# First token tile loaded in halves over two DMA queues, mixing factors turned between filler products, decay and bias turned by VectorE

## The chip, the cores and the metric

The kernel runs on one core of a Trainium2 chip. A core has five engines with a queue of instructions each: TensorE (PE in the profile; its weight loads are PEld), VectorE (DVE), ScalarE (ACT), GpSimd (POOL) and SyncE (SP). Engines run side by side and wait for each other by semaphores. TensorE multiplies and writes to PSUM[...]. Data come from HBM by DMA. A DMA is issued by an engine's queue, here that of SyncE or ScalarE, and is carried out by 16 DMA engines that both queues share.

The metric is the device time of one execution in microseconds; lower is better.

## The reference

The input `x` has 4 sequences of 1024 tokens with 512 features, in float32. One layer is computed: a normalization, a recurrent "time mix" part and a feed-forward part, both on the normalized tokens, added to `x`. Cut to what matters:

```python
xn = layernorm(x)

# time mix
xx = concat([xn[:, 1:2], xn[:, :-1]], axis=1) - xn     # token before, minus token
k = (xn + xx * time_mix_k) @ Wk.T                      # 512 -> 704
r = (xn + xx * time_mix_r) @ Wr.T                      # 512 -> 704
w = exp(-exp(time_decay))
state_t = state_{t-1} * w + relu(k_t)                  # along the tokens
a = layernorm((state_t * r_t) @ Wv.T) * ln_gamma + ln_beta

# feed-forward
D = gelu(float16(xn) @ W0.T + bias0).astype(float16)   # 512 -> 2048
E = (D @ W1.T + bias1).astype(float16)                 # 2048 -> 512
out = x + a + E
```

In the kernel `time_mix_k` and `time_mix_r` are the mixing factors, `time_decay` and `bias0` the decay and the bias of the title. Each is a vector along features or hidden units, stored in HBM as a row; the kernel needs it as a column, one value in each partition, so it loads rows and turns them.

## The kernel before

The 4096 tokens are worked on in 8 blocks of 512 tokens. Within a block, features and hidden units lie on the partitions and tokens along the free axis, so a block's normalized tokens must be turned (transposed) first. A block is then the `k` and `r` products (`pk`, `pr`, five chunks of 128 hidden units and a half chunk), the scan over the tokens on VectorE, the product with `Wv` (`po`), and 16 chunks of the feed-forward part (`pd` up, `pe` down). A block's normalization and turning run beside the block before it; TensorE then has products from one block to the next.

The first block has nothing to run beside. `first_inputs` (line 233) does its start by hand: TensorE, VectorE and ScalarE run there in the order in which the lines are written (`tc.manual_schedule`, line 311). The block is cut into four slices `s` of 128 tokens, one for each of the four tiles that `load_x` loads. The steps are:

- **Loads.** `load_x` (line 80) issues on SyncE's queue two tiles of 128 tokens (256 KB each), then four pieces of `wk`, the first three chunks' columns (line 98), then the other two tiles. The rest of `wk` follows (line 128), then `wr` (130), the first pieces of `W0` (150), `Wv`, gamma, beta and `bias1` (180 to 185), and the next block's tiles (87). Each DMA of a queue waits until an earlier one has released its semaphore; there are 8 of these, handed out in turn over both queues. On ScalarE's queue are the mixing factors (123, 124), 4 rows each into `mix_rows`, then the decay (125, 126) and the bias (127), 22 rows in all, into `late_rows`. After these, ScalarE loads the table of the square root (315).
- **Filler.** `busy(n)` (line 249) issues `n` products of zeros into a PSUM tile that nobody reads, `idle`. A float32 product takes two passes on TensorE, so ten of them are 20 matmul records.
- **First slice.** VectorE takes mean and variance of slice 0 (263, 264), ScalarE the root (265). VectorE then does the statistics of slice 1 (266), the reciprocal (267) and the normalization of slice 0 in two pieces, 128 columns and 384 (`normalized`, line 206). Slice 1 gets its statistics in full at line 270 and its root from GpSimd (196, 197).
- **Factors.** TensorE turns `mix_rows` into the PSUM tile `small` after the ten fillers (317). ScalarE copies it to `mix_sb` and makes one minus the factors (319, 320).
- **Turning and mixing.** `turned(s)` (line 276) turns a slice with four transposes into the PSUM tiles `pt`. `mixed` makes the mixed input `xk` of each feature chunk `c`: ScalarE scales (292), VectorE adds the token before (297). `products` (307) then multiplies each chunk with three chunks of `wk`; these go into `pk_0` to `pk_2`.
- **Late rows.** TensorE turns `late_rows` into `small` too, after `turned(0)` (322). ScalarE copies them to `late_sb` after the first slice's mixing (338) and makes `w` from the decay with two exponentials (340, 341), ahead of which it loads another table.

The loop over the slices (327 to 343) puts the turning of slice `s + 1` ahead of the last chunk's products of slice `s`, and the statistics of slice `s + 2` at the end of slice `s`. After it come the `r` inputs of all 512 tokens (345), and from there on a scheduler sets the order, with a few waits that the code adds.

Of the kernel before, what the change touches and what calls it, by code (L numbers as in the profile page):

```python
# [10 lines left out]
F32 = mybir.dt.float32  # L11
# [4 lines left out]
P = 128  # L16
# [4 lines left out]
def time_mix_and_gelu_ffn(  # L21
# [26 lines left out]
    nc = tc.nc  # L48
# [4 lines left out]
    NS = TB // P  # L53
    NC = C // P
    NN = N // P
    Q = 32


    NF = HID // P
    H0 = NF * P  # L60
    HF = P // 2
# [3 lines left out]
    def pool(name, bufs, **kw):  # L65
        return ctx.enter_context(tc.tile_pool(name=name, bufs=bufs, **kw))
# [4 lines left out]
    const = pool("const", 1)  # L71
# [8 lines left out]
    def load_x(i, amid=lambda: None):  # L80

        b, t0 = blocks[i]
        xs = one.tile([P, NS, C], F32, tag="x", name=f"x_{i}")
        for s in range(NS):
            if s == NS // 2:
                amid()
            nc.sync.dma_start(xs[:, s, :], x[b, t0 + s * P : t0 + (s + 1) * P, :])
        return xs


# [5 lines left out]
    def load_wk(cols):  # L96
        for c in range(NC):
            nc.sync.dma_start(wk_sb[c][:, cols], wkT[c * P : (c + 1) * P, cols])

    x_now = load_x(0, lambda: load_wk(slice(0, FIRST * P)))  # L100
    ident = const.tile([P, P], F32, name="ident")
    make_identity(nc, ident)
    nhalf = const.tile([P, NS], F32, name="nhalf")
    nc.vector.memset(nhalf, -0.5)


    eps_sb = const.tile([P, 1], F32, name="eps_sb")
    nc.vector.memset(eps_sb, EPS)

# [2 lines left out]
    rest_sb = const.tile([P, 2 * NC], F32, name="rest_sb")  # L112
    mk_sb, mr_sb = mix_sb[:, :NC], mix_sb[:, NC:]
    ND = NF + 1
    late_rows = const.tile([ND + NN, P], F32, name="late_rows")
    nc.vector.memset(late_rows[:, HF:], 0.0)
    late_sb = const.tile([P, ND + NN], F32, name="late_sb")
    w_sb, b0_sb = late_sb[:, :ND], late_sb[:, ND:]

    def rows(ap):  # L120
        return ap.rearrange("(c p) -> c p", p=P)

    nc.scalar.dma_start(mix_rows[:NC], rows(mix_k))
    nc.scalar.dma_start(mix_rows[NC:], rows(mix_r))
    nc.scalar.dma_start(late_rows[:NF], rows(decay[:H0]))
    nc.scalar.dma_start(late_rows[NF:ND, :HF], decay[H0:].rearrange("(c p) -> c p", p=HF))
    nc.scalar.dma_start(late_rows[ND:], rows(bias0))
    load_wk(slice(FIRST * P, HID))
    for c in range(NC):
        nc.sync.dma_start(wr_sb[c], wrT[c * P : (c + 1) * P, :])  # L130
# [61 lines left out]
    def rstd_of(var, name):  # L192

        n = var.shape[1]
        r = two.tile([P, n], F32, tag=f"rstd{n}", name=name)
        nc.gpsimd.tensor_scalar_add(r, var, EPS)  # L196
        nc.gpsimd.tensor_tensor(r, r, nhalf[:, :n], ALU.pow)
        return r

    def stats_of(mv, s, src, name):  # L200
        st6 = two.tile([P, 6], F32, tag="st6", name=name)
        nc.vector.bn_stats(st6, src)  # L202
        nc.vector.bn_aggr(mv[:, s, :], st6)  # L203

    def normalize(dst, src, mean, rstd):
        nc.vector.tensor_scalar(dst, src, mean, rstd, ALU.subtract, ALU.mult)
# [21 lines left out]
    def product(dst, w, cols, src, c):  # L228
        return nc.tensor.matmul(  # L229
            dst, w[c][:, cols], src, start=(c == 0), stop=(c == NC - 1)  # L230
        )

    def first_inputs(xs, behind):

        pts = [ps_e.tile([P, TB], F32, tag="pe", name=f"pt_0_{c}") for c in range(NC)]
        idle = ps_mm.tile([P, TB], F32, tag="mm", name="idle")
        small = ps_mm.tile([P, TB], F32, tag="mm", name="small")  # L240
        mix_t, late_t = small[:, : 2 * NC], small[:, 2 * NC : 2 * NC + ND + NN]
        mv = two.tile([P, NS, 2], F32, tag="mv", name="mvx_0")
        dev = two.tile([P, NS], F32, tag=f"rstd{NS}", name="rx_0")
        rstds = {}
        xk = one.tile([P, NC, TB], F32, tag="xk", name="xk_0")

        zeros = nc.const_aps.tensor(0.0, (P, P), F32)

        def busy(n):

            for _ in range(n):
                nc.tensor.matmul(idle[:, :P], zeros, zeros, start=True, stop=True)  # L252

        def stats(s):
            stats_of(mv, s, xs[:, s, :], f"stx_0_{s}")
            rstds[s] = rstd_of(mv[:, s, 1:], f"rx_0_{s}")

        def first_stats():


            sixes = [two.tile([P, 6], F32, tag="st6", name=f"stx_0_{s}") for s in range(2)]
            rstds[0] = dev[:, :1]
            nc.vector.bn_stats(sixes[0], xs[:, 0, :])
            nc.vector.bn_aggr(mv[:, 0, :], sixes[0])
            nc.scalar.activation(rstds[0], mv[:, 0, 1:], AF.Sqrt, bias=eps_sb)
            nc.vector.bn_stats(sixes[1], xs[:, 1, :])
            nc.vector.reciprocal(rstds[0], rstds[0])
            normalized(0, slice(0, P))
            normalized(0, slice(P, C))
            nc.vector.bn_aggr(mv[:, 1, :], sixes[1])  # L270
            rstds[1] = rstd_of(mv[:, 1, 1:], "rx_0_1")

        def normalized(s, cols=slice(0, C)):
            normalize(xs[:, s, cols], xs[:, s, cols], mv[:, s, 0:1], rstds[s])

        def turned(s):
            for c in range(NC):
                nc.tensor.transpose(  # L278
                    pts[c][:, s * P : (s + 1) * P], xs[:, s, c * P : (c + 1) * P], ident
                )  # L280

        def mixed(kind, c, a, b):

            src = pts[c]
            if kind == 0:
                dst = part = xk[:, c, :]
            else:
                part = two.tile([P, TB], F32, tag="xx", name=f"ar_0_{c}")
                dst = xnT[:, c, 1:]
            j = kind * NC + c  # L290
            m = mix_sb[:, j : j + 1]
            scaled = nc.scalar.activation(
                part[:, a:b], src[:, a:b], AF.Identity, scale=rest_sb[:, j : j + 1]
            )

            def add(a, b, before):
                return nc.vector.scalar_tensor_tensor(
                    dst[:, a:b], src[:, before], m, part[:, a:b], ALU.mult, ALU.add
                )

            if a == 0:

                add(0, 1, slice(1, 2))
                a = 1
            return scaled, add(a, b, slice(a - 1, b - 1))

        def products(c, part):
            for h, pk in enumerate(pks):
                product(pk[:, part], wk_sb, slice(h * P, (h + 1) * P), xk[:, c, part], c)

        with tc.manual_schedule(
            engines={nc.scalar.engine, nc.vector.engine, nc.tensor.engine}
        ):

            nc.scalar.activation(dev[:, 1:2], eps_sb, AF.Sqrt)
            busy(10)
            nc.tensor.transpose(mix_t, mix_rows, ident[: 2 * NC, : 2 * NC])  # L317
            first_stats()
            nc.scalar.copy(mix_sb, mix_t)
            nc.scalar.activation(rest_sb, mix_t, AF.Identity, bias=1.0, scale=-1.0)  # L320
            turned(0)
            nc.tensor.transpose(late_t, late_rows, ident[: ND + NN, : ND + NN])  # L322
            busy(1)
            pks = [
                ps_mm.tile([P, TB], F32, tag="mm", name=f"pk_0_{h}") for h in range(FIRST)
            ]
            for s in range(NS):
                tokens = slice(s * P, (s + 1) * P)
                for c in range(NC):
                    if c == NC // 2 and s + 1 < NS:  # L330
                        normalized(s + 1)
                    mixed(0, c, tokens.start, tokens.stop)
                for c in range(NC):
                    if c == NC - 1 and s + 1 < NS:
                        turned(s + 1)
                    products(c, tokens)
                if s == 0:
                    nc.scalar.copy(late_sb, late_t)

                    nc.scalar.activation(w_sb, w_sb, AF.Exp)  # L340
                    nc.scalar.activation(w_sb, w_sb, AF.Exp, scale=-1.0)
                if s + 2 < NS:
                    stats(s + 2)
            for c in range(NC):
                scaled, added = mixed(1, c, 0, TB)

        behind.enter_context(tc.issue_after(scaled.ins))
        behind.enter_context(tc.issue_after(added.ins))

        def first_x16s():  # L350
            x16s = []
            for c, pt in enumerate(pts):
                x16 = four.tile([P, TB], F16, tag="x16", name=f"x16_0_{c}")
                nc.scalar.copy(x16, pt)
                x16s.append(x16)
                nc.scalar.copy(last[:, c, :], pt[:, TB - 1 :])
            return x16s

        return first_x16s, xk, pks
# [367 lines left out]
```

## Time and profile before

| | |
|---|---|
| median of 3 runs | 936.43 us (936.25 to 936.46) |
| the profiled execution | 936.47 us |
| its span, first to last instruction | 934.7 us |
| TensorE busy | 930.4 us |
| VectorE busy | 501.6 us |
| ScalarE busy | 162.1 us |
| DMA, mean over the span | 114 GB/s, 106.54 MB |

The span is what the trace covers; the 1.8 us beside it are ahead of the first instruction and behind the last. In the views of the profile, a line of the timeline gives start, length, engine, source line, operation and operands, the count of instructions that it merges, and in brackets how long the engine sat idle before and what ended that. L252 is line 252 of the kernel. The chain of waits is the work that ended last, followed back from the last instruction. A matmul record lasts from its first read to its modelled end, and consecutive ones overlap; the distance from start to start is the pace. Records of DMA-issuing instructions (SPq, ACTq) cover the issue alone, not the transfer; the DMA views give the time to landing.

The busy time of TensorE includes the filler products at the start.

### The profile page before, as it was taken

The numbers are of one execution on the slowest core, as the hardware profiler recorded it, in microseconds if no ns is written. First come the engines' busy times: TensorE is split into PE (matmuls) and PEld (weight loads), VectorE is DVE, ScalarE is ACT, GpSimd is POOL, SyncE is SP. The second block draws the span as 40 slices with busy tenths as digits, with TensorE's granted clock in tenths as the row PEclk, the third lists the DMA queues.
The fourth block names the chain that finished last, engine by engine and source line by source line (L and its number), as shares of the span: only waits on it lengthen the run. The fifth ranks groups of instructions, "written<-read, shape, count | busy, mean of one in ns | idle before, by whom it ended". The sixth has DMA issues, their size and how long they took to land.

```text
span 934.7 us, 9382 instructions
## 1 busy us (share of the span) xinstructions
PE 930.4 (100%) x3520; PEld 593.9 (64%) x3520; DVE 501.6 (54%) x879; ACT 162.1 (17%) x274; POOL 54.3 (6%) x130
## 2 busy tenths in 40 slices
PE   9999999999999999999999999999999999999998
PEld 8478644885448854588545884458844588445687
DVE  6798384733846348453484525755357552552513
ACT  6254100220012200112001220112200121001011
POOL 1100010000100001000010000100001000000100
PEclk9999999999999999999999999999999999999999
DMA  9568620443204432054320543105431044310243
GB/s 300 185 202 277 229 90 0 149 144 113 90 1 157 148 101 90 0 170 146 102 79 0 180 143 114 59 1 189 149 113 46 11 147 141 107 45 1 67 151 120
DMA packets 40729, 106.54 MB, mean 114 GB/s; under 512 B 4559, under 2 KB 6636, under 8 KB 40684
## 3 DMA queue, kind: packets, MB, share of 16 engines
q1 hardware_dynamic: 40624, 105.92, 34.7%
q8 instruction: 28, 0.46, 0.2%
q14 instruction: 17, 0.14, 0.0%
q10 hardware_dynamic: 60, 0.02, 0.0%
HBM read 89.14 MB, written 16.78 MB: 113 GB/s over the span
## 4 chain that ended last, share of the span: by engine, by line
PE 99%; DVE 0%; issue 0%
PE pd L550 25%; PE pe L566 24%; PE po L476 15%; PE pk L229 15%; PE pr L229 15%; PE pkr L447 3%; PE po L487 2%; PE idle L252 1%; DVE z L534 0%; PE pt L278 0%; DVE e L584 0%; DVE e L529 0%; PE small L322 0%; PE small L317 0%
## 5 line engine op out<-in xcount | busy, mean ns | idle before, releaser
L566 PE MATMUL pe<-w,d 128*128 128x512 f32 x1008 | 246.8, 389 | 0.0
L566 PEld LDWEIGHTS pe<-w,d 128*128 128x128 f32 x1008 | 189.1, 188 | 39.8 <-DVE d L560 0.7
L550 PE MATMUL pd<-xf,w0h 128*128 128x512 f32 x512 | 202.7, 396 | 0.0
L550 PE MATMUL pd<-xf,w0l 128*128 128x512 f32 x512 | 199.3, 389 | 0.0
L560 DVE CAST d<-d 128x512 fp32r<-128x512 f16 x128 | 54.3, 425 | 190.3 <-ACT d L558 188.9
L558 ACT ACTIVATE d<-pd,late_sb 128x512 f16<-128x512 f32 x128 | 87.8, 687 | 346.9 <-PE pd L550 346.9
L229 PE MATMUL pk<-xk,wk 128*128 128x512 f32 (+1 forms) x392 | 144.8, 515 | 0.0
L229 PE MATMUL pr<-xnT,wr 128*128 128x512 f32 x320 | 143.7, 592 | 0.0
L476 PE MATMUL po<-wv_sb,g 128*128 128x512 f32 x320 | 140.8, 595 | 0.0
L229 PEld LDWEIGHTS pk<-xk,wk 128*128 128x128 f32 x392 | 67.5, 190 | 70.9 <-issue 70.6
L550 PEld LDWEIGHTS pd<-xf,w0h 128*128 128x128 f32 x512 | 96.1, 188 | 22.5 <-issue 2.7
L550 PEld LDWEIGHTS pd<-xf,w0l 128*128 128x128 f32 x512 | 96.1, 188 | 21.7 <-issue 1.9
L229 PEld LDWEIGHTS pr<-xnT,wr 128*128 128x128 f32 x320 | 60.5, 189 | 76.4 <-issue 76.4
L476 PEld LDWEIGHTS po<-wv_sb,g 128*128 128x128 f32 x320 | 60.1, 190 | 76.0 <-issue 75.4
L223 DVE STREAM_TRANSPOSE xnT<-x 32x512 f32<-32x512 f32 x112 | 78.7, 702 | 1.9
L401 ACT ACTIVATE rk<-pk 128x512 f32<-128x512 f32 x40 | 23.9, 597 | 234.6 <-PE pk L229 228.9
L202 DVE BATCH_NORM_STATS2 sty<-po 128x6 f32<-128x512 f32 x32 | 22.0, 689 | 68.7 <-PE po L487 67.8
L403 DVE TENSOR_TENSOR_SCAN st<-late_sb,carry,rk 128x512 f32<-128x512 f32 (+1 forms) x24 | 30.7, 1279 | 40.9 <-ACT rk L401 40.9
L429 DVE TENSOR_TENSOR g<-st,pr 128x512 f32<-128x512 f32 x40 | 27.4, 684 | 34.5 <-PE pr L229 33.7
L403 DVE TENSOR_TENSOR_SCAN st<-late_sb,rk 128x512 f32<-128x512 f32 (+1 forms) x24 | 29.2, 1218 | 29.3 <-ACT rk L401 29.3
L196 POOL TENSOR_SCALAR ry<-mvy 128x1 f32<-128x1 f32 x32 | 11.4, 356 | 499.6 <-DVE mvy L203 499.6
L401 ACT ACTIVATE rk<-kr 64x512 f32<-64x512 f32 x8 | 5.0, 630 | 163.1 <-DVE kr L456 163.1
(76 smaller groups left out, 494.5 us busy)
## 6 DMA issues: line engine op xcount, KB each, us to landing
w<-w1d SPq DMA_DIRECT2D x111, 512.0 KB, 3.3
x<-in_L_attn_x SPq DMA_DIRECT2D x32, 256.0 KB, 4.1
w1d<-w SPq DMA_DIRECT2D x16, 512.0 KB, 3.0
xres<-in_L_attn_x SPq DMA_DIRECT2D x32, 256.0 KB, 2.7
out<-z SPq DMA_DIRECT2D x28, 256.0 KB, 2.6
w0raw<-in_L_ffn_W SPq DMA_DIRECT2D x16, 256.0 KB, 4.1
w1raw<-in_L_ffn_W SPq DMA_DIRECT2D x16, 256.0 KB, 4.2
wr<-in_L_attn_Wr SPq DMA_DIRECT2D x4, 352.0 KB, 4.9
```

The costliest lines, as they stand in the source:

```text
L202: nc.vector.bn_stats(st6, src)
L223: nc.vector.transpose(dst[i * Q : (i + 1) * Q, :, :, j, :], src[j * Q : (j + 1) * Q, :, :, i, :],)
L229: return nc.tensor.matmul(dst, w[c][:, cols], src, start=(c == 0), stop=(c == NC - 1))
L401: state["relu"] = nc.scalar.activation(rk[:hw], pk, AF.Relu)
L403: nc.vector.tensor_tensor_scan(st[:hw], w_sb[:hw, h : h + 1].to_broadcast([hw, TB]), rk[:hw], 0.0 if t0 == 0 else carry[:hw, h : h + 1], A ...
L429: nc.vector.tensor_mul(g[:, h, :], st, pr)
L447: nc.tensor.matmul(out_, w[c][rows, H0:], src, start=(c == 0), stop=(c == NC - 1),)
L476: nc.tensor.matmul(pos[s], g[:, h, s * P : (s + 1) * P], wv_sb[:, h, :], start=(first and h == 0), stop=(not first and h == NF - 1),)
L550: nc.tensor.matmul(pd, w[c][:, cols], xf[:, c, :], start=(c == 0 and w is w0h), stop=(c == NC - 1 and w is w0l),)
L558: state["gelu"] = nc.scalar.activation(d16, pd, AF.Gelu, bias=b0_sb[:, n : n + 1])
L560: state["cast", n] = nc.vector.tensor_copy(d, d16)
L566: nc.tensor.matmul(pe[s] if sum_ is None else sum_, d[:, s * P : (s + 1) * P], w1[part][:, cols], start=(n == first and part == 0), stop=( ...
```

## The change

1. `load_x` issues the very first tile as two DMAs of 64 rows, the first on SyncE's queue and the second on ScalarE's. All other tiles stay whole on SyncE's.
2. The decay and the bias move from ScalarE's queue to SyncE's, behind the four tiles of the first block and the first `wk` pieces, ahead of the rest of `wk`. The mixing factors stay on ScalarE's, behind the half tile.
3. The mixing factors are turned after seven filler products, and two more follow.
4. `late_rows` becomes 32 rows, all set to zero first, and is no longer turned by TensorE. VectorE turns it in four 32x32 pieces straight into `late_sb`, after the mixing of the third slice. The two exponentials and their table move there too, and ScalarE's copy goes.

```diff
         for s in range(NS):
             if s == NS // 2:
                 amid()
-            nc.sync.dma_start(xs[:, s, :], x[b, t0 + s * P : t0 + (s + 1) * P, :])
+
+            queues = (nc.sync, nc.scalar) if i == s == 0 else (nc.sync,)
+            rows = P // len(queues)
+            for q, queue in enumerate(queues):
+                r0 = q * rows
+                first = t0 + s * P + r0
+                queue.dma_start(xs[r0 : r0 + rows, s, :], x[b, first : first + rows, :])
...
     ND = NF + 1
-    late_rows = const.tile([ND + NN, P], F32, name="late_rows")
-    nc.vector.memset(late_rows[:, HF:], 0.0)
-    late_sb = const.tile([P, ND + NN], F32, name="late_sb")
-    w_sb, b0_sb = late_sb[:, :ND], late_sb[:, ND:]
+    late_rows = const.tile([Q, P], F32, name="late_rows")
+    nc.vector.memset(late_rows, 0.0)
+    late_sb = const.tile([P, Q], F32, name="late_sb")
+    w_sb, b0_sb = late_sb[:, :ND], late_sb[:, ND : ND + NN]
...
     nc.scalar.dma_start(mix_rows[:NC], rows(mix_k))
     nc.scalar.dma_start(mix_rows[NC:], rows(mix_r))
-    nc.scalar.dma_start(late_rows[:NF], rows(decay[:H0]))
-    nc.scalar.dma_start(late_rows[NF:ND, :HF], decay[H0:].rearrange("(c p) -> c p", p=HF))
-    nc.scalar.dma_start(late_rows[ND:], rows(bias0))
+    nc.sync.dma_start(late_rows[:NF], rows(decay[:H0]))
+    nc.sync.dma_start(late_rows[NF:ND, :HF], decay[H0:].rearrange("(c p) -> c p", p=HF))
+    nc.sync.dma_start(late_rows[ND : ND + NN], rows(bias0))
     load_wk(slice(FIRST * P, HID))
...
-        mix_t, late_t = small[:, : 2 * NC], small[:, 2 * NC : 2 * NC + ND + NN]
+        mix_t = small[:, : 2 * NC]
...
             nc.scalar.activation(dev[:, 1:2], eps_sb, AF.Sqrt)
-            busy(10)
+            busy(7)
             nc.tensor.transpose(mix_t, mix_rows, ident[: 2 * NC, : 2 * NC])
+            busy(2)
             first_stats()
             nc.scalar.copy(mix_sb, mix_t)
             nc.scalar.activation(rest_sb, mix_t, AF.Identity, bias=1.0, scale=-1.0)
             turned(0)
-            nc.tensor.transpose(late_t, late_rows, ident[: ND + NN, : ND + NN])
             busy(1)
...
                     products(c, tokens)
-                if s == 0:
-                    nc.scalar.copy(late_sb, late_t)
+                if s == NS - 2:
+                    for f in range(0, P, Q):
+                        nc.vector.transpose(late_sb[f : f + Q], late_rows[:, f : f + Q])
 
                     nc.scalar.activation(w_sb, w_sb, AF.Exp)
                     nc.scalar.activation(w_sb, w_sb, AF.Exp, scale=-1.0)
```

`Q` is 32, `NS` and `NC` are 4, `NF` is 5, `NN` is 16. Compiled, the engines' orders differ from before in these places alone, but for two VectorE instructions near 31 us of the trace that swap (`w0l` of the first group's third piece, line 138, and the product `g` of the second chunk, line 429).

## The prediction

> **What bounds the kernel now.** The page comes first. TensorE (PE) is busy for the whole span, so a change that takes nothing from TensorE's stream can only move the point from which that stream runs without a gap, or open a gap later.
>
> ```profile
> span 934.7 us, 9382 instructions
> PE 930.4 (100%) x3520; PEld 593.9 (64%) x3520; DVE 501.6 (54%) x879; ACT 162.1 (17%) x274; POOL 54.3 (6%) x130
> ```
>
> But "busy" counts filler. The chain of waits of the first 40 us shows it (start, length, what):
>
> ```profile
> 0.76 4.61 PE idle L252 x20
> 5.37 0.20 PE small L317
> 5.57 1.04 PE pt L278 x4
> 6.62 0.23 PE small L322
> 6.84 0.45 PE idle L252 x2
> 7.29 2.01 PE pk L229 x18
> ```
>
> Until about 7.1 us PE does filler (L252), two small transposes and the first tile's four (L278). From the first `pk` product on, all is work. The price of a pass is in the same lines: 20 filler passes take 4.61 us (0.23 each; 0.213 apart once running), 18 passes of `pk` take 2.01 (0.112 each). PE works at half its pace until about 7.0 us: in a narrow window of the timeline the last slow filler pass starts at 6.77, and the next starts at 7.02 and 7.13.
>
> The timeline of the first 12 us says who sets 7.13:
>
> ```profile
> 0.72 0.86 SPq L87 DMA_DIRECT2D x<-in_L_attn_x  x2
> 1.30 0.25 ACTq L124 DMA_DIRECT2D mix_rows<-in_L_attn_time_mix_r  x1
> 3.28 0.70 DVE L263 BATCH_NORM_STATS2 stx<-x 128x6 f32<-128x512 f32 x1 [2.31 <-DMA x<-in_L_attn_x]
> 4.11 0.66 DVE L266 BATCH_NORM_STATS2 stx<-x 128x6 f32<-128x512 f32 x1
> 4.87 0.73 DVE L206 TENSOR_SCALAR x<-x,mvx,rx 128x128 f32<-128x128 f32 x2
> 5.30 0.27 PE L317 MATMUL small<-ident,mix_rows 8*128 8x8 f32 x1
> 5.50 1.11 PE L278 MATMUL pt<-ident,x 128*128 128x128 f32 x4
> 6.08 1.14 ACT L292 ACTIVATE xk<-pt,rest_sb 128x128 f32<-128x128 f32 x4 [0.23 <-PE pt L278]
> 6.48 0.86 DVE L297 SCALAR_TENSOR_TENSOR xk<-pt,mix_sb,xk 128x1 f32<-128x1 f32 x4 [0.79 <-ACT xk L292]
> 8.75 0.69 DVE L202 BATCH_NORM_STATS2 stx<-x 128x6 f32<-128x512 f32 x1 [0.19 <-DMA x<-in_L_attn_x]
> ```
>
> The first statistics wait for the tile (3.28). The first normalized piece is done at 5.22 (4.87 + 0.35), but PE starts turning it at 5.50, since filler (to 5.30) and the factors' transpose (L317) stand ahead: 0.26 us of slack on PE's side. The last line matters later: the third tile's statistics already wait for their DMA.
>
> ```profile
> DMA to landing us min/median/max: 2.5/2.8/4.6
> ```
>
> That is the view of tile `x` in 0 to 5 us: issued at 0.72, 1.17 and 4.12, the tiles land near 3.26, 3.93 and 8.73.
>
> The DMA view in narrow windows shows how the two queues share the engines (queue, packets): q10 is ScalarE's queue.
>
> ```profile
> q10 hardware_dynamic: 8, 0.00, 2.4%
> q10 hardware_dynamic: 8, 0.00, 6.0%
> q10 hardware_dynamic: 10, 0.00, 4.5%
> ```
>
> These are 1.6 to 1.95, 2.5 to 2.65 and 3.15 to 3.4 us; in 1.95 to 2.5 and 2.65 to 3.15 q10 has none. So a small DMA of ScalarE is served about once for each large DMA of SyncE: k factors at 1.7, r factors near 2.55, when the first tile is through, decay near 3.25, when the second is.
>
> **What the Trainium skill says.** "DMA: Bandwidth & Descriptors", section Rules for kernel authors: of two transfers to disjoint partition halves it says "Don't bother — they serialize", and what two queues save is issue time. Its section Queues, rings and completion order has each DMA engine go round the queues, a packet from each in turn; the q10 counts above agree. "TensorE: Matmul & The Clock Gate", Part 1, gives half the clock until an activity window of about 3.4 us was busy, at a phase that does not start with the kernel; the 0.213 and 0.112 us agree, and the switch near 7.0, 6.2 us after the first pass, allows more than one window. "Vector Engine (DVE) Microarchitecture Reference", 3.8: a 32x32 transpose streams one element per cycle and lane. The trace has only 512-element ones, about 0.716 us from start to start.
>
> **The change part by part.**
>
> *Filler and factors on PE.* 10 fillers become 7, the factors' transpose, then 2. It would start at 5.30 - 6 x 0.213 = 4.02 if the factors are there. It takes 0.20 and 2 fillers (4 passes) 0.85: PE is free near 5.1, and the tile's transpose waits for VectorE alone: 5.22 + 0.03 = 5.25 in place of 5.50. The second transpose waits for the other piece (5.60). So the four end 0.14 to 0.25 earlier, ScalarE's L292 and VectorE's L297 up to 0.26.
>
> *The late transpose on PE goes* (0.23 us from its start, with 0.14 ahead of it): PE comes to the one filler (0.43) and to `pk` 0.37 earlier, on top of the above. `pk` then waits for its operand (L297's first two, done at 6.96 before).
>
> *The tile in halves.* 128 + 128 KB on two queues instead of 256 on one; engines are busy from 1.75 on either way, so the transfer keeps its length of about 0.9. Bounds for its landing: 0.35 earlier (better use of each engine by two queues, 0.2 less issue) to 0.25 later (ScalarE's first DMA took 0.55 to issue for 4 rows, SyncE's 128 rows 0.39). I take 0.1 earlier. More would not pay in full: the second tile's statistics (L266) stand ahead of the reciprocal on VectorE and landed at 3.93 for a start at 4.11, 0.16 of room.
>
> *The factors' DMAs* become second and third on ScalarE's queue, behind 64 rows. By the turns above, the r factors land between 3.6 (ScalarE's half goes first) and 4.55 (SyncE's first: half, half, second tile, k, first weights, r). Needed: 4.02. At 4.2 PE is free at 5.25, which costs nothing; at 4.55 it is free at 5.6 and nothing is gained there.
>
> *Sum to `pk`.* With 0.1 and 0.26: L297's pair ends at 6.60, `pk` starts near 6.63 instead of 7.13. But PE is slow until 7.0: what it does in 0.37 us there is 1.75 passes, worth 0.20 at the full pace, and the 0.13 of filler between 7.00 and 7.13 is saved: gain about 0.33. Next, the third tile: its landing at 8.7 isn't moved by PE; statistics and aggregation (L202, L203) then end so that the next L297 could start at 9.58 instead of 9.85 at the earliest: a cap of 0.27, 0.1 more or less with the landing. I take 0.28.
>
> *The late rows.* Three small DMAs (0.31, 0.27, 0.34 us) move from ScalarE to SyncE, ahead of four `wk` and four `wr` loads and all behind. SyncE's waits are for earlier transfers, so mostly order changes; the last `wr`, issued at 9.45, landing near 14.3, comes up to 1 us later; needed at 19.5. Next block's tile, landing at 26.4, may come 0.5 later: VectorE waits 3.27 us for it with L429 behind, which frees the PSUM buffer of the `pk` at 29.81 at 27.69: 1.7 us of room. ScalarE's table load and two exponentials move from 7.3 to after 13.82 (end of the third slice's L292); it is idle until:
>
> ```profile
> 15.91 0.88 ACT L292 ACTIVATE xk<-pt,rest_sb 128x128 f32<-128x128 f32 x3 [2.09 <-PE pt L278]
> ```
>
> Load 1.28 to 15.10. The four VectorE transposes follow L297 at 14.58: estimate: at one element per cycle and the 0.96 GHz of "Trainium Kernel Development and Optimization", NeuronCore Architecture, 512 elements are 0.533 of the 0.716 us and 0.183 is fixed, so 32 elements take 0.033 + 0.183 and four 0.86, done at 15.4. Exponentials 0.21 + 0.24: last start 15.65, end 15.86. Hidden by 0.05 to 0.15; if each transpose took 0.3, L292 would start 0.2 late, and PE with it, since PE waits for that L297. I take 0, bounds 0 to 0.25. One copy less on ScalarE and the larger memset are under idle time.
>
> **Sum.** The profiled execution took 936.47 us, 934.7 of it span; the median of the runs is 936.43, so the same. 936.43 - 0.28 = 936.15, given as 936.2.
>
> **Rivals.**
> - *Forecast* (0.53): 936.2, own range 935.8 to 936.4.
> - *Factors late or exponentials late* (0.20): r factors at 4.55 let PE start turning at 5.6, 0.1 later than before; the late transpose's 0.37 pays that back: 936.4, no change. For it: three q10 DMAs with one turn each. Against: ScalarE's first packet came at 1.69, SyncE's at 1.75.
> - *Slow pace kept for one window more* (0.16), the other side: while PE waits for the factors, 3.9 to at most 4.6, and for the tile, its activity falls; below what the window asks for, the switch comes 3.4 us later, at 10.4. From 6.63 to 10.4 PE does 17.7 passes, where before 29 were done by then: 11.6 x 0.112 = 1.3 slower: 937.7. It decides once the gap is over some half microsecond. Against: fillers and transposes of before had gaps of about 0.5 in that stretch too.
> - *More gained* (0.06): the halves land 0.35 earlier with all tiles, or the pace rises earlier: 935.7.
> - *Loads late* (0.05): `wr` or the next tile past their room, 1 to 3 us: 937.5 to 939.5.
>
> About 0.2% (1.9 us) is what a measurement of this kernel can tell from no change. Only the last rival and an extreme of the third reach past it on the slow side: 0.04; nothing but an error reaches it on the fast side: 0.02. Range for 8 in 10: 935.7 to 937.3, which leaves out most of the slow-pace case and the late loads.
>
> **What would show it.** Right: L278 starts near 5.15 to 5.3, `pk` near 6.6 to 6.8, passes 0.112 apart from 7.0 on, the wait of L202 for its DMA longer than 0.19, L292 of the fourth slice straight after PE, `pr` products near 19.2 in place of 19.5. Wrong: L317 after 4.5; passes 0.213 apart past 7.2; an idle stretch of ScalarE behind the transposes at 15.9; PE gaps at 19 to 30 us.

## The result, and the profile after

| | before | after |
|---|---|---|
| median beside each other | 936.44 us (936.25 to 936.67, 12 runs) | 938.72 us (937.54 to 939.73, 12 runs) |
| the profiled execution | 936.47 us | 937.54 us |
| its span | 934.7 us | 935.7 us |

The ratio is 1.0023, with a 95% interval of 1.0015 to 1.0031: slower, by about 2.2 us. The profiled execution is the shortest of its twelve, so its trace shows only 1.07 us of the loss; a second one, `e8_after_again` below, shows more.

The timeline of TensorE in the first 9.5 us of after (start, duration, engine, line, operation, out<-in, shapes, count, and the idle time before with what ended it):

```profile
0.76 3.33 PE L259 MATMUL idle<-const-float32-0.0 128*128 128x128 f32 x14 [0.76 <-PEq L718]
4.78 0.24 PE L324 MATMUL small<-ident,mix_rows 8*128 8x8 f32 x1 [0.69 <-DMA mix_rows<-in_L_attn_time_mix_r]
...
5.97 1.09 PE L285 MATMUL pt<-ident,x 128*128 128x128 f32 x4
6.85 0.64 PE L259 MATMUL idle<-const-float32-0.0 128*128 128x128 f32 x2
7.47 2.20 PE L236 MATMUL pk<-xk,wk 128*128 128x128 f32 x14
```

The last pass of the seven fillers starts at 3.67 and, at 0.213 us a pass, is through at 3.88; the factors' transpose (L324) starts at 4.78. That is a hole of 0.9 us, ended by the DMA of the `r` factors. The 0.69 in brackets counts from the modelled end of the last pass; holes below are counted by the pace, unless the text names the bracket. Turning starts at 5.97 in place of 5.50, and `pk` at 7.47 in place of 7.13. The last line holds a second loss: 14 products in the 2.03 us to the edge of the window. The first two starts are 0.34 us apart; from there on it is 0.213 until 8.3 and 0.112 after, where before the change all of these products ran at 0.112. So TensorE is 0.34 late when `pk` starts and 0.81 late by 8.4. It stays about 0.8 late to its last instruction (931.77 in place of 930.92).

Where the factors were is in the chain of waits of after, 0 to 40 us (start, us, what):

```profile
0.72 0.57 ACTq L93
...
1.33 0.98 ACTq L130
...
2.34 2.30 DMA mix_rows<-in_L_attn_time_mix_r
```

ScalarE's queue issues its half of the tile for 0.57 us, the `k` factors for 0.98, and only then, at 2.34, the `r` factors, which before were issued at 1.30. They land at 4.65.

The tile itself, in the view of tile `x` in the first 4.5 us of after (duration in ns as min/median/max, then first and last start):

```profile
L93 SPq DMA_DIRECT2D x<-in_L_attn_x x3: 430/567/569, 0.7 to 4.1; - x3
L93 ACTq DMA_DIRECT2D x<-in_L_attn_x x1: 572/572/572, 0.7 to 0.7; - x1
...
L270 DVE BATCH_NORM_STATS2 stx<-x x1: 695/695/695, 3.8 to 3.8; 128x6 f32<-128x512 f32 x1
...
DMA to landing us min/median/max: 2.6/3.0/4.4
```

and of before:

```profile
L87 SPq DMA_DIRECT2D x<-in_L_attn_x x3: 387/421/430, 0.7 to 4.1; - x3
```

A load of 64 rows took 0.57 us to issue, and so did the whole tile behind it on SyncE; before, the first tile took 0.39 and the second 0.42. SyncE's half landed 2.6 us after its issue began, near 3.3, as the whole tile did before; ScalarE's half took 3.0 and landed near 3.75. The first statistics (L270) need both and start at 3.77, not at 3.28.

VectorE's timeline at the next block's first statistics, and at the copy of `kr`, of after:

```profile
28.03 0.69 DVE L209 BATCH_NORM_STATS2 stx<-x 128x6 f32<-128x512 f32 x1 [4.09 <-DMA x<-in_L_attn_x]
...
48.15 0.69 DVE L463 COPY kr<-pkr 128x512 f32<-128x512 f32 x1
```

and of before:

```profile
26.40 0.70 DVE L202 BATCH_NORM_STATS2 stx<-x 128x6 f32<-128x512 f32 x1 [3.27 <-DMA x<-in_L_attn_x]
...
47.34 0.69 DVE L455 COPY kr<-pkr 128x512 f32<-128x512 f32 x1 [0.38 <-PE pkr L447]
```

The tile lands 1.63 us later. Before, VectorE waited 0.38 us for TensorE at `kr`; now it is late itself. In after that costs nothing more, as TensorE is 0.8 late too; the first experiment shows what it costs when TensorE is not.

Last, the late rows, in the timelines of VectorE and ScalarE of after:

```profile
15.39 0.84 DVE L346 STREAM_TRANSPOSE late_sb<-late_rows 32x32 f32<-32x32 f32 x4
```

```profile
16.50 0.21 ACT L349 ACTIVATE late_sb<-late_sb 128x6 f32<-128x6 f32 x1
16.72 1.14 ACT L299 ACTIVATE xk<-pt,rest_sb 128x128 f32<-128x128 f32 x4
```

The exponentials end at 16.71, just before the fourth slice's L299. This starts 0.31 us after the first transpose of its slice (16.41), exactly as before (15.60 to 15.91), so the exponentials are hidden.

### The profile page after: what moved, and what is told of

It is laid out like the page before. It is cut to its first block, busy times and chain, and to the rows that moved or that the text cites. A ratio compares the mean times of both kernels' runs of the same rounds, so it can differ in the third digit from the quotient of the medians.

```text
span 935.7 us, 9379 instructions
## 1 busy us (share of the span) xinstructions
PE 930.6 (99%) x3517; PEld 593.8 (63%) x3517; DVE 502.4 (54%) x883; ACT 162.0 (17%) x273; POOL 54.3 (6%) x130
## 4 chain that ended last, share of the span: by engine, by line
PE 99%; DVE 0%; DMA 0%; ACTq 0%; issue 0%
PE pd L558 25%; PE pe L574 24%; PE po L484 15%; PE pk L236 15%; PE pr L236 15%; PE pkr L455 3%; PE po L495 2%; DVE z L542 0%; DMA mix_rows<-in_L_attn_time_mix_r 0%; PE pt L285 0%; PE idle L259 0%; DVE e L592 0%; ACTq L130 0%; DVE e L537 0%; ACTq L93 0%
## 5 line engine op out<-in xcount | busy, mean ns | idle before, releaser
L203 POOL TENSOR_SCALAR ry<-mvy 128x1 f32<-128x1 f32 x32 | 11.4, 356 | 499.3 <-DVE mvy L210 499.3
```

## The experiments

All ran beside the kernel before (medians 936.65, 936.54 and 936.47 us in the three groups that follow). Diffs are against the kernel named; lines of `...` leave code out.

**First group: one part at a time.** `e1_whole_tile`, against after:

```diff
-            queues = (nc.sync, nc.scalar) if i == s == 0 else (nc.sync,)
+            queues = (nc.sync,)
```

> The changed kernel with its first tile whole on SyncE's queue again; all else as changed. Theory A (the two halves slow each other's issue, so the second half and then the factors land late; that delay and the hole it leaves in TensorE's filler are the whole loss): the tile lands near 3.26 us as before, the factors are there before 4.0, the hole is gone, pk starts near 6.8, 936.2 us (0.2 to 0.3 under before) with a spread of runs under 0.6. Rival B (the loss comes from the moved late rows and exponentials): still about 938.5. Rival C (the smaller number of fillers ahead of the factors alone keeps TensorE slow for longer): 937 to 939 with a spread of about 2 us.

Measured: 937.54 us (936.32 to 938.04, 13 runs), ratio 1.0008 (1.0000 to 1.0016). The start is what the prediction had hoped for: factors turned at 4.02, `pk` at 6.83 with its products at 0.112, `pr` at 19.27 in place of 19.50. Yet it is no faster. TensorE's timeline from 51 us on:

```profile
52.38 0.39 PE L558 MATMUL pd<-xf,w0l 128*128 128x512 f32 x1
53.67 1.66 PE L574 MATMUL pe<-w,d 128*128 128x512 f32 x6 [0.91 <-DVE d L568]
```

TensorE waits 0.91 us for VectorE's `d` at its first down product, and goes from 0.23 early to 0.73 late. The chain of waits leads from there back to `kr`, and from `kr` over two loads of `W0` to VectorE's `w0l` at 31.68:

```profile
31.68 0.68 DVE w0l L145
...
32.41 3.38 DMA w0raw<-in_L_ffn_W
...
37.18 4.61 DMA w0raw<-in_L_ffn_W
...
48.87 0.70 DVE kr L464
...
49.65 0.64 ACT rk L409
...
51.52 0.67 DVE w L145
...
53.19 0.44 DVE d L568
...
53.67 2.11 PE pe L574 x8
```

VectorE's timeline shows where the lateness begins: VectorE waited for the next block's tile until 27.30, and the statistics stand in its order ahead of the product `g`, the scan and the `W0` pieces:

```profile
27.30 0.69 DVE L209 BATCH_NORM_STATS2 stx<-x 128x6 f32<-128x512 f32 x1 [4.40 <-DMA x<-in_L_attn_x]
27.91 0.67 DVE L437 TENSOR_TENSOR g<-st,pr 128x512 f32<-128x512 f32 x1
28.50 1.22 DVE L411 TENSOR_TENSOR_SCAN st<-late_sb,rk 128x512 f32<-128x512 f32 x1
```

The lateness does not stay in VectorE's queue, which sits idle for 0.90 us on the way (at 36.46). By the chain, a load of a `W0` piece starts when a `w0l` is done (32.36 and 37.16), and a later `w0l` waits, over ScalarE's `w0h`, for that load. So a late `w0l` makes the loads late too.

`e2_halves_only`, against before, has the halves alone:

```diff
-            nc.sync.dma_start(xs[:, s, :], x[b, t0 + s * P : t0 + (s + 1) * P, :])
+            queues = (nc.sync, nc.scalar) if i == s == 0 else (nc.sync,)
+            rows = P // len(queues)
+            for q, queue in enumerate(queues):
...
+                queue.dma_start(xs[r0 : r0 + rows, s, :], x[b, first : first + rows, :])
```

> The kernel before with the halved first tile alone. Theory A: the ScalarE half lands near 3.75 instead of 3.26 and the chain on VectorE is 0.5 late; ten fillers stand ahead of the factors, so the hole in TensorE is only some 0.3 us: 936.9 to 937.5, less than the changed kernel's 938.7, with a smaller spread. Rival B (late rows and exponentials): no more than before, 936.4. If two queues did help: under 936.4.

Measured: 939.62 us (939.12 to 940.83, 6 runs), ratio 1.0033 (1.0021 to 1.0044). First statistics at 3.88, ten fillers through at 5.2, turning at 6.54. TensorE's timeline has a hole of 1.32 (in brackets), and 18 products take 3.88 us, 0.213 apart until 11.4:

```profile
6.54 0.94 PE L283 MATMUL pt<-ident,x 128*128 128x128 f32 x4 [1.32 <-DVE x L211]
...
7.95 3.88 PE L234 MATMUL pk<-xk,wk 128*128 128x128 f32 x18
```

So the halves alone, expected to lose less than the whole change, lose at least as much: 3.0 us by the medians against 2.3, though the two intervals overlap.

`e3_gap_only`, against before, opens a hole and moves no load:

```diff
-            busy(10)
+            busy(7)
```

> The kernel before with seven fillers instead of ten: data arrive as before, but TensorE has nothing to do from about 4.2 to 5.25 us. Theory A2 (the hole in the filler keeps TensorE at half pace past the start of pk): slow passes beyond 7.2 us, 937 to 939 us with a spread of 1 to 2 us, though every data wait is as before. Rival D (late data alone cost the time, the pace is chance): 936.2 to 936.4, spread as before, 0.4.

Measured: 937.66 us (936.63 to 938.17, 13 runs), ratio 1.0008 (1.0000 to 1.0016). TensorE's timeline:

```profile
5.54 1.29 PE L278 MATMUL pt<-ident,x 128*128 128x128 f32 x4 [1.25 <-DVE x L206]
...
7.58 3.16 PE L229 MATMUL pk<-xk,wk 128*128 128x128 f32 x18
```

TensorE idles 1.31 us ahead of turning, which starts about where it did (5.50). Still the products stay 0.213 apart until 9.66, and in the profiled execution TensorE ends 1.4 us late. Three fillers fewer, and no load moved: the hole alone costs the pace. In time that is 1.0 us by the medians, at the edge of what these runs can tell.

`e4_gap_filled`, against after, closes it:

```diff
-            busy(7)
+            busy(11)
             nc.tensor.transpose(mix_t, mix_rows, ident[: 2 * NC, : 2 * NC])
-            busy(2)
```

> The changed kernel with eleven fillers ahead of the factors and none after: the halves and the moved late rows stay, only the hole in TensorE's stream is closed; the first transposes still wait for the late half and begin near 5.97. Theory A2: full pace from about 7.0 as before, pk near 7.4 to 7.5, 936.7 to 936.9 with a spread under 0.6: some 1.9 us of the loss come from the pace. Rival D (late data alone): 938.7 and a spread of 2 us as in the changed kernel, since the data are as late.

Measured: 937.12 us (936.88 to 937.53, 13 runs), ratio 1.0004 (0.9996 to 1.0013). The change's 1.0015 to 1.0031 does not overlap with this: of its 2.2 us about 1.8 are gone. TensorE's timeline:

```profile
7.29 2.25 PE L236 MATMUL pk<-xk,wk 128*128 128x128 f32 x18 [0.25 <-ACT xk L299]
```

With the halves still late (statistics at 3.90) TensorE reaches full pace at 3.97 in this execution and keeps it, and ends 0.29 late. The edit also let the scheduler put the next tile's statistics behind other work on VectorE, so there was no stall at `pe`. That order is not what was saved: in after `pe` starts 0.81 late, no later than the `pk` products by 8.4.

**Second group: loads, order, halves.** `e5_late_back` is `e1_whole_tile` with the three late loads back where they were:

```diff
-    nc.sync.dma_start(late_rows[:NF], rows(decay[:H0]))
+    nc.scalar.dma_start(late_rows[:NF], rows(decay[:H0]))
...
-    nc.sync.dma_start(late_rows[ND : ND + NN], rows(bias0))
+    nc.scalar.dma_start(late_rows[ND : ND + NN], rows(bias0))
```

> The changed kernel with the first tile whole again and the decay and bias loads back on ScalarE's queue; the mixing factors' early transpose and the four VectorE transposes stay. Theory A (the three small loads on SyncE delay every load behind them; the next block's tile lands 0.9 us later, and VectorE, which has its statistics ahead of the next products, delivers everything up to the first gelu later): next tile's first statistics near 26.4 us (27.30 with the whole tile and the loads on SyncE), copy of kr waiting for PE again, no stall at the first down product near 53 us, PE 0.2 to 0.3 us ahead of the kernel before to the end, 0.25 us below it. Theory B (the stall comes from VectorE's own new work, the transposes and the changed order of one w0l piece): tile near 26.4 but the stall of 0.7 to 1 us stays, 0.7 us above the kernel before.

Measured: 937.75 us (936.50 to 938.07, 13 runs), ratio 1.0009 (1.0000 to 1.0017). VectorE's instructions stand in the same order as in `e1_whole_tile`, and the timeline shows the tile earlier by 1.84 us and `kr` waiting for TensorE again:

```profile
25.46 0.70 DVE L209 BATCH_NORM_STATS2 stx<-x 128x6 f32<-128x512 f32 x1 [2.01 <-DMA x<-in_L_attn_x]
...
47.66 0.69 DVE L463 COPY kr<-pkr 128x512 f32<-128x512 f32 x1 [1.97 <-PE pkr L455]
```

The stall at `pe` is gone, so Theory A holds and B falls: with this order on VectorE, the late loads on SyncE made it. The 1.84 is the difference of one pair of executions. Over all in which VectorE waited for this tile, the statistics start at 25.46 to 27.24 with these loads on ScalarE's queue (before, `e2`, `e3`, `e5`, `e10`) and at 26.96 to 28.46 with them on SyncE's (after, `e1`, `e8`, `e11`). The time did not follow: `pk` started 0.17 early, but waits for data at 10.1 to 11.9, behind a third tile whose statistics waited for its DMA until 9.14, left TensorE 0.32 late. The runs lie from 936.50 to 936.84 (five) and from 937.23 to 938.07 (eight); the profiled one, 936.84, is of the first five, so what the eight lost is open.

`e6_whole_tile_other_order` is `e1_whole_tile` with the fillers in one group, which changes VectorE's order but not the loads:

```diff
-            busy(7)
+            busy(9)
             nc.tensor.transpose(mix_t, mix_rows, ident[: 2 * NC, : 2 * NC])
-            busy(2)
```

> The changed kernel with the first tile whole and nine fillers ahead of the factors' transpose, none behind it (in place of seven and two). The loads stay on SyncE, but the scheduler now puts the next tile's first statistics behind the scan, the products g and three w0l pieces on VectorE. Theory A with order (a late tile costs only where VectorE's queue has its statistics ahead of other work): the tile lands late, near 27, but nothing waits behind it; the first w0l piece near 25.3, copy of kr waiting for PE, no stall near 53 us, start of the first products 0.2 to 0.3 us earlier than in the kernel before, 0.25 us below it. Rival (the late loads themselves, w0 pieces among them, set the chain): stall of 0.5 to 1 us near 53 us in spite of the order, 0.5 us above the kernel before.

Measured: 936.44 us, ratio 1.0004 (0.9996 to 1.0012). The thirteen runs lie in two groups, seven at 936.25 to 936.44 and six at 937.59 to 937.78. With the late loads on SyncE, VectorE's timeline has the `W0` piece at 26.16, ahead of the statistics:

```profile
25.24 0.66 DVE L436 TENSOR_TENSOR g<-st,pr 128x512 f32<-128x512 f32 x1
...
26.16 0.69 DVE L145 TENSOR_TENSOR w0l<-w0raw,w0h 128x512 fp32r<-128x512 f32 x1
...
29.67 1.28 DVE L209 BATCH_NORM_STATS2 stx<-x 128x6 f32<-128x512 f32 x2
```

No stall follows at `pe`: a late tile costs only where work is queued behind its first reader. The profiled execution is of the second group. It has a hole of 0.47 ahead of turning and products 0.213 apart until 9.25, 1.1 us late in all. So the two groups look like the pace again; the first group was not profiled.

`e7_halves_one_queue`, against after:

```diff
-            queues = (nc.sync, nc.scalar) if i == s == 0 else (nc.sync,)
+            queues = (nc.sync, nc.sync) if i == s == 0 else (nc.sync,)
```

> The changed kernel with both halves of the first tile on SyncE's queue, one after the other; ScalarE's queue begins with the factors, as in the kernel before. Theory C (two queues that issue at the same time slow each other's issue, 0.57 us each in place of 0.39, and ScalarE's factors come behind a half): halves issued at 0.72 and 1.1 to 1.2 with 0.35 to 0.45 us each, tile landed by 3.4 to 3.6, factors near 4.0, hole on PE under 0.3 us, no pass at half pace after 7.5 us, 0 to 0.3 us from the kernel before. Theory D (a transfer of 64 rows is itself slower to issue or to land): each half takes 0.5 us or more to issue or the first statistics start at 3.75 or later all the same, and the first products start later than in the kernel before.

Measured: 938.95 us (937.54 to 940.37, 20 runs), ratio 1.0022 (1.0015 to 1.0029). The view of tile `x`, 0 to 4.5 us:

```profile
L93 SPq DMA_DIRECT2D x<-in_L_attn_x x4: 430/575/579, 0.7 to 4.5; - x4
L270 DVE BATCH_NORM_STATS2 stx<-x x1: 694/694/694, 4.1 to 4.1; 128x6 f32<-128x512 f32 x1
```

Alone on one queue each half still took 0.57 to 0.58 us to issue. Theory C, that two queues issuing at once slow each other, falls as the cause of the long issue, and D holds. The factors were turned at 4.02, but the first statistics waited for the tile until 4.07, and TensorE stood still ahead of turning (1.06 in the bracket of its line).

`e8_after_again` is the changed kernel once more.

> The changed kernel once more, for a second profiled execution. If the hole on PE ahead of the factors decides how long TensorE stays at half pace, and the phase of its window varies from one execution to the next, then the hole is again 0.8 to 1.0 us, and the time follows the last pass at half pace: 937.5 us with it near 8.4 us, 939 us with it between 10 and 12 us. If the spread of the changed kernel's times comes from somewhere else, the half pace ends near 8.4 us whatever the time.

Measured: one run, 938.23 us. TensorE's timeline:

```profile
5.08 0.24 PE L324 MATMUL small<-ident,mix_rows 8*128 8x8 f32 x1 [1.00 <-DMA mix_rows<-in_L_attn_time_mix_r]
...
7.77 1.93 PE L236 MATMUL pk<-xk,wk 128*128 128x128 f32 x8
```

The hole is 1.2, the last slow product is near 9.46, and TensorE ends 1.56 late. The hole came out larger than expected, and the time lies between the two that were named.

**Third group: holes closed, halves cut the other way.** `e9_whole_filled` and `e10_late_back_filled` are `e1_whole_tile` and `e5_late_back` with eleven fillers ahead of the factors and none behind:

```diff
-            busy(7)
+            busy(11)
             nc.tensor.transpose(mix_t, mix_rows, ident[: 2 * NC, : 2 * NC])
-            busy(2)
```

> The first tile whole, the late loads on SyncE, eleven fillers ahead of the factors' transpose and none behind it, so that PE has no hole ahead of the first turning. The scheduler puts the next tile's statistics behind other VectorE work, as with nine fillers. Theory (the runs at 937.6 of the version with nine fillers kept half pace one window longer, because of its hole of 0.47 us; its other runs, at 936.3, are what the change is worth without a hole and without a stall): hole under 0.2 us, all or nearly all runs in one group within 0.4 us, 0.1 to 0.3 us below the kernel before, none 1.2 us above it. Rival (the two groups come from something other than the hole, such as the loads behind the late rows): two groups again, a third or more of the runs 1 us above the others.

> As the kernel above, but with the decay and bias loads back on ScalarE's queue; the next tile's statistics stand ahead of the other VectorE work. Theory: the tile lands before 26.5 us, no stall near 53 us, hole under 0.2 us, one group of runs, 0.1 to 0.3 us below the kernel before. Rival (as above): two groups 1 us apart.

Measured: 936.61 us (936.30 to 936.97) and 936.75 us (936.40 to 937.01), 13 runs each, ratios 1.0000 (0.9992 to 1.0008) and 1.0002 (0.9994 to 1.0011). Each is one group within 0.7 us, none 1.2 us above the kernel before. So the second group of runs went with the hole. The hoped 0.1 to 0.3 us below the kernel before did not come. In `e9` eleven fillers push the factors' transpose to 5.72, `pk` then waits for the mixed input and starts 0.28 late. In the profiled execution of `e10` (936.42 us) `pk` starts 0.18 early and TensorE ends 0.06 early; why its median is not lower is open.

`e11_halves_by_columns`, against after:

```diff
-            rows = P // len(queues)
+            cols = C // len(queues)
+            r0 = t0 + s * P
             for q, queue in enumerate(queues):
...
-                queue.dma_start(xs[r0 : r0 + rows, s, :], x[b, first : first + rows, :])
+                part = slice(q * cols, (q + 1) * cols)
+                queue.dma_start(xs[:, s, part], x[b, r0 : r0 + P, part])
```

> The changed kernel with the two halves cut by columns: 128 rows of 1 KB on each queue in place of 64 rows of 2 KB. Theory (a first transfer of 64 rows takes longer to issue): each half takes 0.35 to 0.45 us to issue on SyncE, the next tile's load too; first statistics at 3.3 to 3.6 us. Rival (any first tile that is cut, or any small first transfer, is slow to issue): 0.55 us or more again, first statistics at 3.7 or later.

Measured: one run, 937.44 us. The view of tile `x`, 0 to 4.5 us:

```profile
L93 SPq DMA_DIRECT2D x<-in_L_attn_x x4: 394/425/430, 0.7 to 4.4; - x4
L93 ACTq DMA_DIRECT2D x<-in_L_attn_x x1: 409/409/409, 0.7 to 0.7; - x1
L270 DVE BATCH_NORM_STATS2 stx<-x x1: 695/695/695, 3.5 to 3.5; 128x6 f32<-128x512 f32 x1
```

128 rows of 1 KB issue in 0.39 and 0.41 us, and the statistics start at 3.54, as with a whole tile. So the 0.57 us come with the cut by rows, not with two queues or with a first load of half the size. The factors, still behind a half, were turned at 4.46: a hole of 0.59, and the pace rose at 8.5.

No version measured faster than the kernel before.

## Why the prediction was wrong

Two terms of the sum failed. The tile and the factors came later than their bounds, which opened a hole in TensorE's stream; and the sum to `pk` let the pace rise at 7.0 whatever the hole. The second cost more. A third term, the room given to the late rows, was wrong too but cost nothing in after.

**The tile in halves** is the term that failed first. The prediction took 0.1 earlier, with bounds of 0.35 earlier and 0.25 later. On two queues the first statistics start at 3.77, 3.88, 3.88 and 3.90 (after, `e8`, `e2`, `e4`), and with the tile whole at 3.28 to 3.60 (before and six variants). The means, 3.86 and 3.48, are 0.38 apart; after against before is 0.49, as the 3.28 on which the prediction built was the earliest of the seven. The late bound came from comparing ScalarE's long issue of 4 rows with SyncE's of 128, and the early one assumed that 64 rows cost less than 128; they cost 0.57 against 0.39. The Trainium skill's "DMA: Bandwidth & Descriptors", Rules for kernel authors, says that the two halves serialize, which was quoted. The landings agree: 3.3 for the first half and 3.75 to 3.87 for the second (after, `e4`, `e8`). That two queues save issue time was counted on, and the traces show the reverse for halves by rows. How 0.18 more of issue becomes 0.38 at the landing is open.

**The factors' DMAs.** The late end given was 4.55. They landed at 4.65, and in the second execution their transpose started at 5.08. The missing term is the issue: 0.57 for the half and 0.98 for the `k` factors ahead of the `r` factors (0.76 to 0.98 behind a half of 64 rows, 0.59 behind one of 128, 0.55 as the first of the queue). The prediction counted turns of the DMA engines, not the time on the issuing queue.

**Sum to `pk`.** 6.63 was expected, 7.47 came. The pass count there used a full pace from 7.0 on, as before. That was the largest error: `e4` closes the hole, leaves the tile late, and loses only 0.4 us of the 2.2. The prediction had the right mechanism as a rival, "Slow pace kept for one window more", at 0.16, with 937.7. The whole family of traces settles how it works. Times below are worked out from the starts of single passes: the moment at which their spacing changes, and what of the 3.41 us ahead of it, or of the 3.41 before or after these, no pass fills (0.213 us each at half pace, 0.112 at full). In before, `e5`, `e9` and `e10`, and for the rise in `e7`, that moment is known only to about 0.2 us.

```
kernel    idle time in one 3.41 us window    pace at the window's end
e10       0.00 (1.6 to 5.0)                  rises
e9        0.14 (2.69 to 6.10)                rises
before    0.33 (3.54 to 6.95)                rises
after     0.49 (4.91 to 8.32)                rises
e1        0.66 (2.51 to 5.92)                rises
e6        0.68 (2.42 to 5.84)                stays slow
e11       0.75 (1.68 to 5.09)                stays slow
after     0.90 (1.50 to 4.91)                stays slow
e8        1.37 (2.63 to 6.04)                stays slow
e3        1.68 (2.83 to 6.25)                stays slow
e5        1.58 (4.40 to 7.81), pace full     stays full
e4        1.70 (3.97 to 7.38), pace full     stays full
e7        2.10 (4.39 to 7.80), pace full     falls
e2        2.14 (4.62 to 8.04), pace full     falls
```

In `e7` the pace falls at 7.80 and rises at 11.22, a step of 3.42 us; in `e2` it rises at 4.62 and again at 11.46, two such steps, and the fall, between 7.95 and 8.21, fits the 8.04 halfway. The Trainium skill's "TensorE: Matmul & The Clock Gate", Part 1, gives a free-running window of 3413 ns, and the traces agree: with the same passes up to 4.2 us the pace rises at 4.40 in `e5` and at 5.92 in `e1`. For the rest of its rule, that a busy window is needed to rise and an idle one to fall, the traces put sizes, and a window need not be idle throughout for the pace to fall: in these thirteen profiles idle time up to 0.66 us in a window let the pace rise, 0.68 or more kept it down (so close that the bound is only about two thirds of a microsecond), 1.7 left a full pace as it was, and 2.1 took it away. Transposes count as passes here. If they counted as idle, the pace would rise after 1.6 us in before and stay slow after 1.0 in after, so they do not. The rival's "once the gap is over some half microsecond" was near, but it priced one hole of at most 0.7 and gave it too little weight: filler taken from ahead of a load whose time is uncertain is the risk itself. A window's phase differs from execution to execution, so the hole costs more in some: that is the likely reason for the spread of 2.2 us in the change's runs. It is argued, not shown, for those near 939.7, as no such run of it was profiled; `e7` at 939.17 and `e2` at 939.12 show what one would look like.

**The late rows.** The next block's tile "may come 0.5 later", with "1.7 us of room": both were wrong. `e1` against before has it 0.9 later, `e5` against `e1` takes the three loads away again and wins 1.84 (one profile each). And the room was read at the wrong wait: it is not at TensorE's `pk` at 29.81 but VectorE's 0.38 us at `kr` (47.34), 20 us on. The prediction stopped at the first consumer of the product behind the statistics, where `e1` shows the lateness go on over the `W0` pieces and their loads to `kr`. In after this lies under TensorE's own 0.8: the two losses do not add.

**What was right.** *Filler and factors on PE* and *the late transpose goes*: with the factors in time their transpose starts at 4.02 (`e1`), turning 0.08 earlier (the tile was 0.15 later than before), `pk` 0.30, and TensorE was 0.23 ahead at `pr`, for the 0.28 of the sum. That the two figures are so close is in part luck: in this execution the pace rose at 5.92, 1.0 us sooner than in before, which the sum did not count on. The four VectorE transposes took 0.84 us (estimate 0.86), and the exponentials stayed hidden. The third tile's cap did not come into play in after; in `e5` it did.

The forecast of 936.2 needed a tile that lands as before, factors at 4.0 and a next tile in time. The change moved all three loads, and each missed. That 936.2 comes when all three are in time is not shown: the seven lower runs of `e6` (936.25 to 936.44) came nearest, and `e10`, with all three and no hole, measured 936.75 beside 936.47.

## What to carry to other kernels

Count what a queue does while it issues, not only when data move: a load put ahead of small urgent loads delays these by its whole issue time, and a split load can take longer to issue than the whole. Where filler keeps a clock up, a hole is priced by the window it falls in, so filler is best cut only by what the wait behind it surely shortens. When a load comes later, follow its first reader's queue, instruction by instruction, with the loads that this queue releases, to the next place at which that engine waits for the bottleneck engine: the wait there is the room, and it may be 20 us away.

## What was not expected of the hardware

- A load of 64 rows of 2 KB took 0.565 to 0.579 us to issue, one of 128 rows of 2 KB 0.381 to 0.395, one of 128 rows of 1 KB 0.394 to 0.409, each first on its queue or behind a half. The second tile, whole, took 0.57 to 0.83 behind a half by rows and 0.42 behind a whole one or a half by columns. Why is open.
- The profile's row of the granted clock reads 9 throughout, 1.00 from 4 to 8 us of after too, where the passes are 0.213 apart: only the spacing of the passes shows the half pace.
